# Attention layer and state-space scan on one core: maxima of four heads side by side, results taken a step later, and the causal convolution folded into the projection's weights

## The chip, the cores and the metric

The kernel runs on one core of a Trainium2 chip. The metric is the device time of one execution in microseconds (us); three executions of the kernel before gave 13804.61, 13823.3 and 13835.7 us, so the median is 13823.3 us. One more execution was taken with the hardware profiler; all rows shown here are from that one.

The engines are named as in the profile: PE is TensorE's matrix product and PEld its load of stationary weights, DVE is VectorE, ACT is ScalarE, POOL is GpSimd, and SP is SyncE, which issues the DMAs of this kernel. Each engine works through its own queue in order. PSUM, the memory into which products go, has eight banks of 128 partitions by 512 float32.

## The reference, cut to what matters

There are 16 samples of 256 channels by 32 x 32 positions (L = 1024), in float32. Each goes through two layers, each with a residual and a group norm before it.

```python
# layer 0: attention, 4 heads of 32
tok = gn(x) + pos_embedding
q, k, v = split(layernorm(tok) @ w_qkv)
attn = softmax(q k^T * 32**-0.5)              # 1024 x 1024 for each head
tok = (attn v) @ w_out + b_out + tok
tok = gelu(layernorm(tok) @ w_ff1 + b_ff1) @ w_ff2 + b_ff2 + tok
x = x + tok

# layer 1: a selective scan, 512 inner channels, 64 states
xp = gn(x) + rel_h + rel_w
ctx = sigmoid(conv3(xp, gate_w) + gate_b)     # dense convolution along positions
u, z = split(xp @ in_proj_w.T)
u = silu(causal_conv4(u, conv_w) + conv_b)    # each channel alone, 4 taps
dt, Bm, Cm = split(u @ x_proj_w.T)
delta = softplus(dt @ dt_proj_w.T + dt_proj_b)
h[t] = exp(delta[t] * A) * h[t-1] + delta[t] * u[t] * Bm[t]   # 512 x 64 states
y[t] = sum over states of h[t] * Cm[t]
x = x + ((y + u * D) * silu(z)) @ out_proj_w.T * ctx
```

## The kernel before, in words

**The scan sets the frame.** The 512 x 64 states of a sample are cut into 256 *units* (list `units`, L805). A unit is two scans of 128 partitions by 512 positions on VectorE (`scan`, L864). Each needs, ahead of it, a decay: a product on TensorE into a PSUM tile `a` (L851) and an exponential on ScalarE (L854), and an input: a DMA of `dub` (L832), 512 KB as it is repeated over partitions, and a product on POOL (L842). Loads are issued six units ahead, POOL's products four, decays two; `a` has four PSUM banks (pool `aps`), so the decays of a unit wait for the scans of two units earlier. Every eight units `outputs` sums over the states with 128 small products into `yb` (L901) and turns the result (L913).

**Preparation runs beside the scan.** While sample b is scanned, a chain of Python generators issues the work of other samples: `first_norm(b + 1)`, `gate_and_store(b - 1)`, `attention_layer(b + 1)` and `scan_inputs(b + 1)`, in this order. Each `yield w` ends a step of weight w. The loop over units (L946) adds a fixed share of the total weight for each unit and issues as many steps as are due. So a weight has no duration: it says how many units, and with them how much of the scan's work, are placed in each engine's queue before the next step's work. `add_manual_dep` at the end (L1001) keeps every engine's queue except SP's in this written order; SP's DMAs are ordered by the scheduler. The first sample is prepared alone, before the first scan (0 to 392 us); the last `gate_and_store` comes after the last scan.

**PSUM beside the scan.** `psum()` (L98) gives preparation the two banks of pool `mm`; pool `accp` has one bank (`av`), used by attention's sums. While the first sample is prepared alone, `psum()` takes turns through `mm` and `aps`.

**The parts that the change touches.**
- `group_norm` (L225) and `layer_norm` (L266): sums or means by products with `avg` on TensorE, then Ln and Exp on ScalarE, then a product on VectorE in a later step (L262, L301). Means of the two halves (L270) are used by VectorE (L277) one step later.
- `attention_layer` (L332): for each pair of heads, `query_key` (L363) projects q and k to rows 0-31 and 64-95 of `qa` and `ka`; 16 double steps compute scores `s_ps` (L408) of 128 queries by 512 keys for each head of the pair, and VectorE takes their maxima (L399) in the next step. The negated maxima are turned into rows by products with one column (`row_ps`, L420) and become row 32 of `qa`, against a row of ones in `ka`, so that the scores `st_ps` (L444) come with the maximum taken off. Then follow exponentials (L452) and the sums with the values (L432).
- `scan_inputs` (L537): z (L580), the tanh of silu and a product (L569) one step later; u (L601), copied to `up`, three taps on VectorE (L615; the fourth is the scale of a ScalarE copy, L607), a tanh and a product (L655); between them the dense gate (L630, L634); then x_proj (L667) and softplus with its split into bfloat16 pieces (L684 to L736).
- `gate_and_store` (L743): output projection `m_ps` (L789), finished by two VectorE operations (L776, L778) half a double step later.
- `spread_c` (L873): once for each half of a sample's positions, eight ScalarE copies (L880) into `cd`, which POOL sets to zero first (L876), once a sample.

## Time and profile before

| what | value |
|---|---|
| median of three executions | 13823.3 us |
| the profiled execution | 13784.86 us |
| its span, first to last instruction | 13782.7 us |
| mean granted TensorE clock | 0.732 |
| busy: DVE, PE, POOL, ACT | 88%, 81%, 76%, 59% |
| before the first scan | 392 us |
| scans of the first sample | 805 us |
| scans of samples 2 to 15 | about 847 us each |
| scans of the last sample, nothing prepared beside it | 677 us |
| one scan of 512 positions (L864) | 1201 to 1261 ns |
| one tap (L615), 192 in all | 1567 ns |
| one reduction of scores (L399), 1024 in all | 678 ns |
| DMA traffic | 2804 MB, 201 GB/s of HBM traffic over the span |

How to read the profile: a row of groups gives line, engine, operation, the tiles written and read, how often, busy time, mean duration, and the idle time of the engine just before with what ended it. A row of waits gives the instruction that waited, what it waited for, the total in us, how many times, the longest. A row of windows gives the length of a stretch and the busy time of each engine in it, then the share of TensorE's clock that was granted (1.00 is full speed), the share of the DMA engines in use, and GB/s. A float32 product stands in the profile as two records. The duration of a matmul is modelled at its end, and matmuls overlap, so TensorE's busy time says that it had work, not that it was at its peak.

### The profile page before, as it was taken

The page shows a single profiled execution, that of the slowest core. Times are in us where ns is not written, and L with a number is a line of the kernel's source. Part 1 is how long each engine was busy: PE and PEld are TensorE (multiplying, and loading weights), DVE is VectorE, ACT ScalarE, POOL GpSimd, SP SyncE. Part 2 cuts the span into 40 slices and gives each one's busy share as a digit, 9 for nine tenths or more (in the row PEclk, how much of TensorE's full clock was granted, in tenths as well). Part 3 has the DMA queues.
Part 4 walks back from the last instruction along what each step waited for, and adds up shares of the span by engine and source line. Part 5 has one row for each costly group of instructions (what it writes and reads, how often), then busy time and mean ns, then how long its engine had stood idle before and what let it go on. Part 6 is the DMA issues. An engine that isn't in the chain of part 4 may idle for free. (4 is left out here: it accounts for less than half of the span.)

```text
span 13782.7 us, 435036 instructions
## 1 busy us (share of the span) xinstructions
PE 11113.2 (81%) x185744; PEld 5728.7 (42%) x185744; DVE 12135.5 (88%) x11699; ACT 8088.7 (59%) x14245; POOL 10477.2 (76%) x8214
## 2 busy tenths in 40 slices
PE   7787878878787787978879788797887978878767
PEld 3344444444444444444444444444444444434434
DVE  3898898898898889888898888889888898888898
ACT  3666665656655565655656655566555655556644
POOL 0787777777787777777777787777777777777788
PEclk8686767867777686876767777677776776867767
DMA  1566566565665656556565565656656565565666
GB/s 55 196 207 230 187 214 208 201 222 196 211 207 199 218 201 223 194 199 218 197 231 186 197 226 191 232 185 202 219 191 230 187 214 205 194 228 187 209 219 223
DMA packets 964174, 2804.18 MB, mean 203 GB/s; under 512 B 138162, under 2 KB 285747, under 8 KB 962228
## 3 DMA queue, kind: packets, MB, share of 16 engines
q1 hardware_dynamic: 962228, 2776.34, 58.8%
q8 instruction: 1452, 23.79, 0.7%
q14 instruction: 494, 4.05, 0.1%
HBM read 2514.18 MB, written 261.62 MB: 201 GB/s over the span
## 5 line engine op out<-in xcount | busy, mean ns | idle before, releaser
L842 POOL TENSOR_TENSOR dub<-dub,bt 128x512 f32<-128x512 f32 x8192 | 10422.4, 1307 | 3254.5 <-DMA dub<-dus 2878.4
L854 ACT ACTIVATE a<-a,acol 128x512 f32<-128x512 f32 x8192 | 5064.9, 660 | 3728.2 <-PE a L851 3689.1
L864 DVE TENSOR_TENSOR_SCAN h<-a,last,dub 128x512 f32<-128x512 f32 x4096 | 4932.9, 1261 | 227.0 <-POOL dub L842 128.8
L864 DVE TENSOR_TENSOR_SCAN h<-a,dub 128x512 f32<-128x512 f32 x4096 | 4700.9, 1201 | 276.7 <-POOL dub L842 186.6
L851 PE MATMUL a<-pieces,pick 48*128 48x512 bf16 x8192 | 2914.9, 480 | 2103.1 <-DVE h L864 2037.8
L901 PEld LDWEIGHTS yb<-h,cd 128*32 128x32 f32 x131072 | 2677.2, 140 | 2166.2 <-issue 1847.3
L901 PE MATMUL yb<-h,cd 128*32 128x64 f32 x131072 | 3090.5, 265 | 160.9 <-DVE yb L891 115.9
L851 PEld LDWEIGHTS <-pick 48*128 48x128 bf16 x8192 | 498.0, 96 | 2507.4 <-issue 2293.2
L408 PE MATMUL s_ps<-ka,qa 32*128 32x512 f32 x2048 | 1115.7, 1009 | 23.2 <-DVE mx L399 15.2
L399 DVE TENSOR_REDUCE mx<-s_ps 128x1 f32<-128x512 f32 x1024 | 654.9, 678 | 279.0 <-PE s_ps L408 278.2
L913 PEld LDWEIGHTS yb<-turn,y 128*16 128x16 f32 x32768 | 418.9, 120 | 960.3 <-ACT y L909 484.6
L909 ACT COPY y<-yb 128x256 f32<-128x256 f32 x1024 | 383.4, 374 | 693.6 <-PE yb L901 688.3
L913 PE MATMUL yb<-turn,y 128*16 128x32 f32 x32768 | 555.2, 216 | 193.8 <-ACT y L909 173.0
L444 PE MATMUL st_ps<-qa,ka 33*128 33x512 f32 x2048 | 590.2, 613 | 25.9 <-ACT pt L452 25.5
L432 PE MATMUL av<-pt,vv 128*64 128x512 f32 x2048 | 572.7, 635 | 4.3 <-ACT sums L390 3.3
L452 ACT ACTIVATE pt<-st_ps 128x512 f32<-128x512 f32 x1024 | 558.9, 609 | 28.8 <-PE st_ps L444 28.4
L408 PEld LDWEIGHTS s_ps<-ka,qa 32*128 32x128 f32 x2048 | 345.4, 274 | 402.3 <-DVE mx L399 221.4
L630 PE MATMUL g_ps<-w,xp 128*128 128x256 f32 x1536 | 475.2, 468 | 0.0
L630 PEld LDWEIGHTS g_ps<-w,xp 128*128 128x128 f32 x1536 | 401.9, 329 | 137.6 <-issue 92.6
L789 PE MATMUL m_ps<-w,xs 128*128 128x256 f32 x1024 | 316.7, 459 | 10.9 <-DVE xs L764 10.9
L921 ACT COPY yo<-yb 128x256 f32<-128x256 f32 x512 | 193.1, 377 | 222.2 <-PE yb L913 219.7
L615 DVE SCALAR_TENSOR_TENSOR u<-up,cwh,u 128x1024 f32<-128x1024 f32 x192 | 300.9, 1567 | 23.8 <-ACT u L607 23.6
(135 smaller groups left out, 7593.8 us busy)
## 6 DMA issues: line engine op xcount, KB each, us to landing
dub<-dus SPq DMA_DIRECT2D x4096, 512.0 KB
dps<-pc SPq DMA_DIRECT2D x384, 128.0 KB
pieces<-dps SPq DMA_DIRECT2D x1024, 48.0 KB
xs<-in_x_dram SPq DMA_DIRECT2D x64, 512.0 KB
xs<-kept SPq DMA_DIRECT2D x64, 512.0 KB
zs<-z SPq DMA_DIRECT2D x64, 512.0 KB
ud<-u SPq DMA_DIRECT2D x64, 512.0 KB
dus<-du SPq DMA_DIRECT2D x64, 512.0 KB
```

What stands on the lines that cost most here:

```text
L399: nc.vector.tensor_reduce(mx[:, e, c, hf : hf + 1], s, AX.X, ALU.max)
L408: nc.tensor.matmul(s, qa[r, ts(c, P)], ka[r, hs(hf)], start=True, stop=True)
L432: nc.tensor.matmul(av[ts(e, 2 * DH)], vv[j // (NJ // 2)][:, j % (NJ // 2), 2 * pair + e, :], pts[e], start=(j == 0), stop=(j == NJ - 1),)
L444: nc.tensor.matmul(s, ka[r, ts(j, P)], qa[r, hs(hf)], start=True, stop=True)
L452: nc.scalar.activation(pt, s, AF.Exp)
L630: nc.tensor.matmul(ps[:, ts(q, C)], xp[k][:, ds(first + t, P, 4)], wg_s[:, k, t, :], start=(i == 0), stop=False,)
L842: nc.gpsimd.tensor_tensor(v, v, blocks[b, t]["bt"], ALU.mult)
L851: nc.tensor.matmul(a, w, pieces[r], start=True, stop=True)
L854: nc.scalar.activation(a, a, AF.Exp, scale=acol[:, at : at + 1])
L864: nc.vector.tensor_tensor_scan(now["h", q % 2][:, 2 * i + e, :], decays[n][e], loaded[n][:, e, :], first, ALU.mult, ALU.add,)
L901: nc.tensor.matmul(yb[ts(g, 32), ts(s, 64)], cd[:, at // 16, ts(c, 32)], hbuf[:, :, at : at + 4], start=(c == 0), stop=(c == 3),)
L913: nc.tensor.matmul(out4[32 * s : 32 * s + 16, half, e], y2[:, 64 * s + e : 64 * s + 64 : 4], turn[:, e], start=True, stop=True,)
```

## The change

1. *Maxima.* `query_key` is gone. q and k of all four heads are projected into `q4` and `k4`, head h in rows 32h to 32h + 31. Each of 32 steps issues four products, one for each head: 32 rows, 64 queries, 512 keys; two heads share a PSUM bank (partitions 0-63 and 64-127), and two banks hold the four. VectorE reduces the two banks in the next step, as before. The maxima are turned by one product, copied, and sent to `qa` by DMA. `qa` and `ka` of each pair are made from `q4` and `k4` by DMA (`spaced`), one to a step. The columns of w_qk are brought in an order that suits this (`bring_qk`). v's products come after the maxima instead of before.
2. *Results a step later.* A third bank (`accp`) joins `mm` through `psum3` for layer norm, z, u and m_ps; z's product, u's product and m_ps are finished one step later than before, and both halves' means are issued before VectorE uses the first. Weights of steps around exponentials are split and raised. `cd` is set to zero once, before everything, and its eight copies are spread over two units. In softplus the steps of the two halves are interleaved in another order.
3. *Convolution.* At the start POOL multiplies u's part of w_in by each of the four taps (halved, as before), and the products go to DRAM (`wcv`). u comes from eight products for each half, over four shifted views of the input, which is padded by three zeros; taps on VectorE and the copy `up` are gone. Each half is two steps of four products. The gate's products move from the convolution's steps to softplus's, in pieces of three.
4. *Room.* The weights' tile loses 1024 columns, and the pool `wide` has eleven buffers instead of ten. A_log is no longer kept.

```diff
-    wide = pool("wide", 10)
+    wide = pool("wide", 11)
...
+    three = cycle((mm, mm, accp))
+
+    def psum3(name):
+        src = next(three) if beside["scan"] else next(alone)
+        return src.tile([P, HL], F32, name=name, tag={mm: "mm", accp: "av"}.get(src, "a"))
...
+    cd = hst.tile([P, TB // 16, P], F32, name="cd", tag="cd")
+    nc.gpsimd.memset(cd, 0.0)
...
+    for d in range(ND):
...
+        t = work("wcs").rearrange("p (k t e) -> p k t e", k=KC, t=CONV)
+        for k in range(KC):
+            nc.gpsimd.tensor_tensor(
+                t[:, k], row[:, ts(d % 2, CONV * P)].rearrange("p (t e) -> p t e", t=CONV),
+                wu[:, k, ts(d, P)].unsqueeze(1).to_broadcast([P, CONV, P]), ALU.mult,
+            )
+        nc.sync.dma_start(wcv[ts(d, P), :], t.rearrange("p k t e -> p (k t e)"))
...
         nc.scalar.activation(v, v, AF.Exp, scale=-0.5)
-        yield 1.5
+        yield 1.2
+        yield 1
...
-        m = mean_of([t[:, hs(0)] for t in src], "ln_m")
-        yield 1
-        q0 = centre(0, m)
-        m = mean_of([t[:, hs(1)] for t in src], "ln_m")
+        m0 = mean_of([t[:, hs(0)] for t in src], "ln_m")
+        yield 0.7
+        m1 = mean_of([t[:, hs(1)] for t in src], "ln_m")
+        yield 0.7
+        q0 = centre(0, m0)
         yield 1.2
-        q1 = centre(1, m)
         vs = [mean_of(q0, "ln_v")]
+        q1 = centre(1, m1)
         yield 1.2
         vs.append(mean_of(q1, "ln_v"))
-        yield 1
+        yield 0.8
...
-        yield 2
+        yield 1.3
+        yield 1
...
+        def spaced(to, src, pair):
+            t = work("sp")
+            for e in range(2):
+                nc.sync.dma_start(t[ds(2 * DH * e, DH)], src[ts(2 * pair + e, DH)])
+            to.append(t)
...
+        for c in range(2 * NJ):
+            for hf in range(2):
+                maxima()
+                for g in range(2):
+                    waiting.append((psum("s_ps"), g, c, hf))
+                for h in range(HEADS):
+                    g, e = divmod(h, 2)
+                    r = ts(h, DH)
+                    nc.tensor.matmul(
+                        waiting[g][0][ts(e, 64)], q4[r, ts(c, 64)], k4[r, hs(hf)],
+                        start=True, stop=True,
+                    )
+                if to_space:
+                    to_space.pop(0)()
+                yield 1.1
...
+        ps = psum("neg_ps", HEADS * NJ)[:, :P]
+        nc.tensor.matmul(ps, neg, ident, start=True, stop=True)
+        yield 1.2
+        negt = small.tile([P, P], F32, name="negt", tag="negt")[: HEADS * NJ]
+        nc.scalar.copy(negt, ps)
+        for h in range(HEADS):
+            pair, e = divmod(h, 2)
+            o = 2 * DH * e + DH
+            nc.sync.dma_start(qas[pair][o : o + 1], negt[ts(pair, 2 * NJ), ts(e, 64)])
+        yield 0.7
...
         for d in range(ND):
             z = work("z")
             for hf in range(2):
-                finish_z()
-                ps = psum("z_ps")
+                finish_z(1)
+                ps = psum3("z_ps")
...
-            for k in range(KC):
+            w = wcs[d].rearrange("p (k t e) -> p k t e", k=KC, t=CONV)
+            ps = psum3("u_ps")
+            for i in range(KC * CONV):
+                k, t = divmod(i, CONV)
                 nc.tensor.matmul(
-                    ps, win_s[:, k, ts(d, P)], body[k][:, hs(hf)],
-                    start=(k == 0), stop=(k == KC - 1),
+                    ps, w[:, k, t], xp[k][:, ds(hf * HL + t, HL)],
+                    start=(i == 0), stop=(i == KC * CONV - 1),
                 )
...
+                if i == CONV - 1:
+                    yield 1.3
+            t = hwork("u_t")
+            nc.scalar.activation(t, ps, AF.Tanh, bias=cbh[:, d : d + 1])
+            nc.scalar.activation(ps, ps, AF.Identity, bias=cbh[:, d : d + 1])
+            ready.append((d, hf, t, ps))
-        def tap(d, t):
-            i = d * CONV + t
-            u = us[d]
-            nc.vector.scalar_tensor_tensor(
-                u, ups[d][:, t : t + L], cwh[:, i : i + 1], u, ALU.mult, ALU.add
-            )
...
-            items = [more(d, *items[0]), begin(d, 1)]
-            yield 1
+            items[0] = more(d, *items[0])
+            yield 0.8
+            items.append(begin(d, 1))
+            rest(*items[0])
+            yield 1.3
             items[1] = more(d, *items[1])
-            rest(*items[0])
-            yield 1.4
+            yield 0.8
             rest(*items[1])
...
+            gate(d // 2, d % 2, 0, 0)
             yield 1.4
...
-                ps = psum("m_ps")
+                ps = psum3("m_ps")
...
-                    if q == 0:
+                    if q == 1:
                         finish()
...
-        if (k, q, i) == (0, 0, 6):
-            spread_c(b, t)
+        if (k, q) == (0, 0) and i in (5, 6):
+            spread_c(b, t, ((0, 1), (2, 3))[i - 5])
```

## Prediction

> **What bounds the kernel now.** I read the busy shares first, then VectorE's waits from the first scan to the last (392 to 13737 us), then one sample cut into stages, then TensorE's clock in the stretch before the first scan, where one kind of work runs alone.
>
> ```profile
> PE 11113.2 (81%) x185744; PEld 5728.7 (42%) x185744; DVE 12135.5 (88%) x11699; ACT 8088.7 (59%) x14245; POOL 10477.2 (76%) x8214
> ```
>
> VectorE is busiest, but 12% of its time is idle. The fifteen samples that carry preparation beside their scan take about 847 us each (805 for the first); the last one, with almost none, took 677 (13060 to 13737). So preparation costs some 170 us a sample, and that is what the change touches. Who keeps VectorE waiting (name waited for: total us, times, longest):
>
> ```profile
> DVE h L864 <- POOL dub L842: 315.5, 287, 9.9
> DVE mx L399 <- PE s_ps L408: 209.5, 215, 2.6
> DVE h L864 <- issue: 177.9, 254, 2.6
> DVE z L569 <- ACT z_t L585: 107.6, 85, 2.7
> DVE gn L262 <- ACT gn_v_ps L259: 101.3, 15, 8.4
> DVE xn L301 <- ACT ln_v L296: 94.7, 30, 4.0
> DVE xn L277 <- PE ln_m L270: 76.6, 28, 4.7
> DVE d_ps L699 <- ACT d_ps L695: 75.4, 89, 1.7
> DVE m_ps L776 <- PE m_ps L789: 69.0, 56, 3.4
> ...
> DVE u L615 <- ACT u L607: 20.2, 15, 1.6
> ```
>
> Divided by 15, the waits of preparation (not L864) come to some 50 us a sample, of which the maxima's 14. Then the sample from 4572 to 5419 us by stages; columns: length, busy us of PE, PEld, DVE, ACT, POOL, granted clock, DMA share.
>
> ```profile
> 4597.00:4656.00 59.00, 32.84 (x672) 17.78 (x672) 50.05 (x44) 27.36 (x52) 48.56 (x35) 0.53 0.78 273
> ...
> 4738.00:4805.00 67.00, 63.91 (x739) 28.41 (x738) 56.43 (x66) 26.38 (x48) 41.80 (x34) 0.53 0.44 139
> ...
> 5181.00:5267.00 86.00, 75.46 (x1153) 48.25 (x1153) 79.35 (x64) 43.73 (x74) 66.48 (x48) 0.92 0.57 189
> 5267.00:5400.00 133.00, 96.55 (x1712) 46.63 (x1711) 124.22 (x128) 96.61 (x163) 91.69 (x75) 0.62 0.62 208
> ```
>
> The first row is the end of the group norm with the gate's first products: VectorE lacks 9 us. The second is a pair's maxima: TensorE is busy 63.9 of 67 at a clock of 0.53, so it bounds, not VectorE. The third is convolution, fourth softplus: VectorE bounds both (79 of 86, 124 of 133). Each part of the change must be priced against its own stage's bound.
>
> **Maxima of four heads side by side.** Counts: before, 32 steps a sample, each two 32-row products and two reductions; after, 32 steps, each four 32-row products of 64 columns and two reductions. Reductions (678 ns) stay 64. If the four products run together, TensorE streams as long per step as now. So all hangs on the clock. Three rows from the stretch where TensorE had nothing else:
>
> ```profile
> 80.00:95.00 15.00, 14.04 (x32) 5.08 (x28) 11.19 (x19) 0.00 (x0) 0.00 (x0) 0.50 0.00 0
> 95.00:99.00 4.00, 3.95 (x19) 2.39 (x20) 0.00 (x0) 0.92 (x2) 0.00 (x0) 0.50 0.00 0
> 99.00:100.00 1.00, 1.00 (x8) 0.64 (x6) 0.00 (x0) 0.23 (x1) 0.00 (x0) 0.63 0.00 0
> 100.00:101.00 1.00, 1.00 (x11) 0.62 (x9) 0.00 (x0) 0.57 (x1) 0.00 (x0) 1.00 0.00 0
> ```
>
> Up to 94 us only s_ps runs, two products on 64 of 128 rows: TensorE is 94% busy and stays at 0.50. From 95.05 to 100.91 only row_ps runs, 128 rows by one column: the clock goes to 1.00 within that stretch, before st_ps starts. The second pair repeats it (0.50 to 174, 0.79 over 174 to 176, row_ps from 170.0 to 176). The Trainium skill ("TensorE: Matmul & The Clock Gate", Part 1) says that the clock follows how busy TensorE was in windows of some 3.4 us. By that rule the maxima's 94% should have been at full clock, occupancy does not change, and the gain here is nothing. The row contradicts it: filled rows decide, filled columns hardly. The new quads fill all 128 rows, so I expect a clock near the 0.96 of the st_ps stretch (4805 to 4867).
>
> That the four really overlap no row shows: before has two row groups at once (a pair starts 7 ns apart), or column groups (yb), never both. The same page (Part 3) states rows and columns compose, 10.6 times for 16 tiles; I take "together". At full clock, 8 units then cost TensorE 8 quads x 1.1 us (half of the pair's 2.08 at half clock, rounded up) + 8.5 for the scan's own (4 x 1.10 yb, 2 x 0.47 turns, 8 x 0.39 decays) = 17.3 us; VectorE 16 scans at 2.33 a pair = 18.6, + 16 reductions x 0.6 = 28.2. VectorE becomes the bound: about 28.7 against 33.5 in the row above (67 for its 16 units) and 30 in the second pair's stretch (4891 to 4921). Over four such groups, and with 32 row_ps products shrunk to one, I take **-9.5 us** a sample; 0 if the clock stays, as far as -14 (all of the wait).
>
> The eight spreading DMAs (128 KB each), four 1-row ones and split w_qk fetches are about 1.3 MB beside some 175 MB a sample; SP issues each in about 0.4 us, already waiting for scans 6692 us. They are hidden as long as st_ps, behind whose wait decays would queue, starts two steps (about 6 us) after the negated maxima are sent: v_ps was moved between.
>
> **Convolution in u's weights.** VectorE loses 12 taps x 1.567 = 18.8 us a sample; the last products change from 4 x 1.48 to 8 x 0.69 (same). TensorE gets 64 products instead of 16. Eight u_ps records (four products; each product is two records) took 3.70 us at full clock (296.85), so 64 cost 59.2 us, 44.4 more. The 27.6 us of gate products (8 times 3.18 + 0.69 less overlap) leave this stage for softplus. The program's order puts 24 products into each 8 units: 22.2 + 8.5 = 30.7 us of TensorE, while VectorE needs 19.2 + 3 x 0.69 = 21.3. **The bound crosses to TensorE.** For the 24 units of the third stage row: 59.2 + 3 z steps x 1.98 + 3 x 8.5 = 90.6 against 86 now; the 8 units after them fall from 28 (5267 to 5295) to about 26, since x_ps (14) stays and gates leave. Sum **+2 us**: the 18.8 us saved do not show. From both sides: -8 (TensorE's pieces overlap, z waits counted below go too) to +12 (decays queue behind a 3.7 us piece and the scan waits). Fetching weights adds four 512 KB DMAs less a 512 KB half of w_in: four more of the size of dub's 256, prefetched a whole d (5.6 of weight, 5 units) ahead.
>
> In softplus 8 gates of 3.4 us at full clock, near 6 at half, lie over 40 units whose TensorE is 96.6 of 133 busy at 0.62. VectorE still bounds: 0, or +5 if decays queue.
>
> **Results taken a step later.** All step weights sum to about 276 after, 281 before, over 247 units: one weight is 0.9 unit, 2.9 us.
> - Group norm: the 6.45 us wait at 4606 is a chain: POOL's L876 memset 3.58, then eight L880 copies 2.45 on ScalarE, then exponentials, two table loads of 1.28. The memset is gone, copies are split over two units, and the step grows by 0.7 of weight (2 us). 6.75 a sample to 1.5, second norm 2.6 to 0.6: -7.2.
> - z: a third PSUM buffer and one more step (2.9) cover waits of at most 2.7: 7.2 to 1, of which 2 lie in the convolution groups counted above: -4.5.
> - Layer norm: means start earlier by 0.4 and 0.7, exponentials get 0.3 more: 5.1 to 2.1 and 6.3 to 4.5: -4.8.
> - m_ps: finished one step later: 4.6 to 0.6: -4.
> - d_ps: slack changes from 1.0 and 1.4 of weight to 0.8 and 0.8, with fewer ScalarE operations ahead: 0, between -4 and +4.
> Together **-20.5**; below by half if the delay is only passed to the scans' own waits (L864, 33 us a sample), which no edit addresses.
>
> **Outside the loop.** Before the first scan: SP now stores four weight tiles, each behind two POOL products of about 1.3 us and the taps' round trip, ahead of x's first fetch (14.3 us today): +20. Maxima alone: 54 us at half clock become VectorE-bound, 32 x 1.29 = 41: -13, row_ps -9. u_ps +44, gates moved into idle TensorE time -28. Sum +14. Last sample: -4.
>
> **Sum.** -9.5 + 2 - 20.5 = -28 a sample; 14 x -28, -24 for the first (no m_ps), -4, +14 = -406 us. The profiled execution took 13784.9 us (span 13782.7), so 13379, 2.95% less. The median shown is 13823.3, 0.28% above it; the same share gives **13,415**.
>
> **Rivals.** *More is gained* (0.20): preparation's waits go wholly and TensorE's groups overlap better, about -46 a sample: 13,150. For it: the waits are short and many. Against: the bound crosses in convolution. *The clock stays or waits pass on* (0.14): no -9.5, half of -20.5, softplus +2: -6 to -15 a sample, 13,600 to 13,740. For it: the page's rule, and 0.5 clock wherever little runs. *Slower* (0.10): quads that share a PSUM bank run one after another, so the clock stays and a step costs four passes, 3.8 us, in place of 2.08: 32 x 1.7 = +54 against -18.5 elsewhere, +36 a sample, about 14,350. It decides once a step costs 0.6 us more than now (18.5 / 32). Against it: yb's four column groups write one bank 7 ns apart.
>
> **Numbers.** Forecast 0.55, own range 13,270 to 13,560. For 8 in 10 I leave out the slower case and the outer part of "more": 13,150 to 13,660. A measurement of this kernel tells about 0.2%. Faster 0.87, same 0.03, slower 0.10.
>
> **What would show it.** Right: clock above 0.85 in the maxima's stretch with VectorE over 93% busy; u_ps stretches with TensorE over 93% and VectorE under 80%; no wait of gn for its exponent over 3 us; m_ps and z waits under 20 us in total. Wrong: s_ps records starting a pass apart rather than nanoseconds, the maxima still near 0.55, or L864's waits for dub or issue growing by what the others lost.

## The result and the profile after

The changed kernel takes 13,620.9 us (four executions, 13,611.9 to 13,629.1) against 13,815.9 us for the kernel before on the same chip (13,804.6 to 13,835.7): ratio 0.9857, 95% interval 0.984 to 0.9874. It is faster by 195 us, where 400 were forecast. The time lies above the forecast's own range (13,270 to 13,560) and inside the wide one (13,150 to 13,660). It also lies in the range of the rival "the clock stays or waits pass on" (13,600 to 13,740), although the clock did not stay. The profiled execution has a span of 13,613.7 us, 169 less than before.

First the busy times of the page, then the rows of its groups that the change touched (line, engine, operation, tiles, shapes, count; busy us, mean ns; idle time just before, and what ended it).

```profile
PE 11139.6 (82%) x188338; PEld 5586.7 (41%) x188338; DVE 11853.9 (87%) x11491; ACT 7820.4 (57%) x13878; POOL 10297.0 (76%) x8207
...
L932 DVE TENSOR_TENSOR_SCAN h<-a,last,dub 128x512 f32<-128x512 f32 x4096 | 4934.3, 1262 | 548.7 <-POOL dub L910 369.5
L932 DVE TENSOR_TENSOR_SCAN h<-a,dub 128x512 f32<-128x512 f32 x4096 | 4707.2, 1203 | 336.2 <-POOL dub L910 223.0
...
L675 PE MATMUL u_ps<-xp,xs 128*128 128x512 f32 x2048 | 976.3, 622 | 21.7 <-DMA xs<-wcv 21.6
L442 PE MATMUL s_ps<-k,q 32*64 32x512 f32 x4096 | 889.8, 728 | 51.8 <-DVE mx L423 49.9
L423 DVE TENSOR_REDUCE mx<-s_ps 128x1 f32<-128x512 f32 x1024 | 645.7, 675 | 22.1 <-PE s_ps L442 22.0
```

VectorE's work fell by 282 us (12,135.5 to 11,853.9), but the span fell by only 169: VectorE now stands idle 113 us longer. The scans (L932, formerly L864) show where: 885 us of idle time stand before them. In the kernel before it was 504 us:

```profile
L864 DVE TENSOR_TENSOR_SCAN h<-a,last,dub 128x512 f32<-128x512 f32 x4096 | 4932.9, 1261 | 227.0 <-POOL dub L842 128.8
L864 DVE TENSOR_TENSOR_SCAN h<-a,dub 128x512 f32<-128x512 f32 x4096 | 4700.9, 1201 | 276.7 <-POOL dub L842 186.6
```

The waits of VectorE between the first scan and the last, in the changed kernel:

```profile
DVE h L932 <- POOL dub L910: 592.5, 339, 6.4
DVE h L932 <- issue: 262.7, 300, 5.5
DVE d_ps L758 <- ACT d_ps L754: 202.1, 120, 5.7
DVE u L664 <- ACT u_ps L683: 117.0, 72, 2.0
DVE xs L828 <- DMA xs<-ud: 72.9, 16, 6.1
...
DVE m_ps L844 <- PE m_ps L857: 24.7, 14, 1.8
...
DVE z L636 <- ACT z_t L651: 16.2, 31, 1.7
...
DVE mx L423 <- PE s_ps L442: 12.3, 23, 1.5
...
DVE gn L301 <- ACT gn_v_ps L297: 3.5, 14, 0.3
```

Every wait that the change aimed at has shrunk: maxima 209.5 to 12.3 us, gn 101.3 to 3.5, z 107.6 to 16.2, m_ps 69.0 to 24.7 (the prediction named under 20 us for m_ps and z). Four others have grown: the scans' own from 493 to 855 us, d_ps from 75.4 to 202.1, u from 20.2 to 117.0, the load of ud from 33.3 to 72.9. Now one sample (4580 to 5412 us) in stages. These rows are the end of the group norm, the maxima, the middle of the convolution, and softplus:

```profile
4605.00:4632.00 27.00, 16.64 (x336) 8.94 (x336) 26.70 (x22) 13.59 (x24) 18.88 (x16) 0.56 0.59 198
...
4743.00:4852.00 109.00, 97.48 (x1605) 36.96 (x1607) 108.85 (x127) 46.58 (x86) 80.52 (x66) 0.89 0.54 181
...
5163.00:5226.00 63.00, 62.33 (x777) 29.12 (x776) 43.14 (x40) 29.01 (x52) 39.30 (x32) 1.00 0.56 181
...
5255.00:5370.00 115.00, 88.18 (x1448) 52.16 (x1447) 102.33 (x107) 85.40 (x143) 79.08 (x64) 0.76 0.62 205
```

In the maxima the clock is 0.89 and VectorE is busy 108.85 of 109 us: the bound crossed from TensorE to VectorE, as forecast. In the convolution it crossed the other way: TensorE 62.33 of 63 us, VectorE 43.14. Averaged over samples 3 to 15, each sample's 256 units cut by unit number into the same stages:

| stage, us a sample | before | after | change | forecast |
|---|---|---|---|---|
| group norm, results stored (units 0 to 47) | 167.0 | 159.7 | -7.3 | -11.2 |
| maxima and attention (48 to 135) | 270.9 | 257.7 | -13.2 | -9.5 |
| layer norms, feed forward, z (136 to 175) | 144.0 | 134.0 | -10.0 | -9.3 |
| convolution (176 to 207) | 114.0 | 123.0 | +9.0 | +2 |
| softplus (208 to 239) | 110.4 | 115.7 | +5.3 | 0 |
| rest | 41.6 | 41.4 | -0.2 | 0 |
| sum | 847.9 | 831.5 | -16.4 | -28 |

The 11.6 us missing stand in convolution and softplus (12.3 together); the other stages give 30.5 where 30.0 were forecast. The cut is by unit number, and the steps do not stand at quite the same units in both kernels: beside the scan of one sample, u's products lie in units 179 to 194 before and 182 to 200 after. So a few microseconds can stand in a neighbouring stage. The first scan comes at 422.9 us (392.7 before: +30, forecast +14), and the first sample's scans take 821 us (805: +16, forecast -24).

### The profile page after: what moved, and what is told of

It is laid out like the page before. It is cut to its first block, busy times and chain, and to the rows that moved or that the text cites. A ratio compares the mean times of both kernels' runs of the same rounds, so it can differ in the third digit from the quotient of the medians.

```text
span 13613.7 us, 440125 instructions
## 1 busy us (share of the span) xinstructions
PE 11139.6 (82%) x188338; PEld 5586.7 (41%) x188338; DVE 11853.9 (87%) x11491; ACT 7820.4 (57%) x13878; POOL 10297.0 (76%) x8207
## 5 line engine op out<-in xcount | busy, mean ns | idle before, releaser
L910 POOL TENSOR_TENSOR dub<-dub,bt 128x512 f32<-128x512 f32 x8192 | 10283.0, 1288 | 3243.4 <-DMA dub<-dus 2846.8
L932 DVE TENSOR_TENSOR_SCAN h<-a,last,dub 128x512 f32<-128x512 f32 x4096 | 4934.3, 1262 | 548.7 <-POOL dub L910 369.5
L932 DVE TENSOR_TENSOR_SCAN h<-a,dub 128x512 f32<-128x512 f32 x4096 | 4707.2, 1203 | 336.2 <-POOL dub L910 223.0
L919 PE MATMUL a<-pieces,pick 48*128 48x512 bf16 x8192 | 2728.5, 452 | 1915.9 <-DVE h L932 1886.8
L966 PEld LDWEIGHTS yb<-h,cd 128*32 128x32 f32 x131072 | 2495.5, 132 | 1834.3 <-issue 1676.3
L966 PE MATMUL yb<-h,cd 128*32 128x64 f32 x131072 | 2889.6, 254 | 71.3 <-issue 67.2
L675 PE MATMUL u_ps<-xp,xs 128*128 128x512 f32 x2048 | 976.3, 622 | 21.7 <-DMA xs<-wcv 21.6
L442 PE MATMUL s_ps<-k,q 32*64 32x512 f32 x4096 | 889.8, 728 | 51.8 <-DVE mx L423 49.9
L510 PE MATMUL st_ps<-sp 33*128 33x512 f32 x2048 | 614.7, 634 | 15.1 <-DMA sp<-negt 7.3
L675 PEld LDWEIGHTS u_ps<-xp,xs 128*128 128x128 f32 x2048 | 380.8, 195 | 490.9 <-issue 447.4
L696 PE MATMUL g_ps<-w,xp 128*128 128x256 f32 x1536 | 558.9, 513 | 9.6 <-ACT g L704 9.6
L442 PEld LDWEIGHTS s_ps<-k,q 32*64 32x64 f32 x4096 | 201.9, 147 | 552.2 <-DVE mx L423 513.3
```

The lines of the kernel that those rows point to most:

```text
L442: nc.tensor.matmul(waiting[g][0][ts(e, 64)], q4[r, ts(c, 64)], k4[r, hs(hf)], start=True, stop=True,)
L510: nc.tensor.matmul(s, ka[r, ts(j, P)], qa[r, hs(hf)], start=True, stop=True)
L675: nc.tensor.matmul(ps, w[:, k, t], xp[k][:, ds(hf * HL + t, HL)], start=(i == 0), stop=(i == KC * CONV - 1),)
L696: nc.tensor.matmul(ps[:, ts(q, C)], xp[k][:, ds(first + t, P, 4)], wg_s[:, k, t, :], start=(k == 0 and t == 0), stop=False,)
L910: nc.gpsimd.tensor_tensor(v, v, blocks[b, t]["bt"], ALU.mult)
L919: nc.tensor.matmul(a, w, pieces[r], start=True, stop=True)
```

## The experiments

**Theory.** The clock in the maxima follows filled rows; the missing gain was lost in softplus's new order and in the convolution's and gates' work on TensorE. **Rivals.** The delays only move the waits on to the scans; or the fetch of the folded weights, not TensorE's work, fills the convolution; or it is only the places of steps against units that shifted. Ratios are against the kernel before, on the same chip.

### The clock: rows filled with zeros

```diff
+                nc.sync.dma_start(ka[2 * DH * e + DH : 2 * DH * (e + 1)], ones)
+                nc.sync.dma_start(qa[2 * DH * e + DH : 2 * DH * (e + 1)], zeros)
...
-                        r = ds(2 * DH * e, DH)
+                        r = ds(2 * DH * e, 2 * DH)
```

The kernel before, with rows 32 to 63 of each head's half of q zero (those of k zero but for one row of ones), so that its scores contract over 64 rows. Work, order and results stay; the two products of a pair now fill 128 rows with half of them nothing.

> The kernel before, with one thing changed: rows 32 to 63 of each head's half of qa and ka hold zeros (ones in row 32 of ka) while the maxima are taken, and the scores' products contract over 64 rows instead of 32. Same number of products, same columns, same result; four row groups are filled instead of two. Theory 'rows decide the clock': granted clock in the maxima's stretches rises from about 0.55 to over 0.8, VectorE's wait for s_ps falls from 14 us a sample to under 3, time falls by 8 to 12 us a sample, 120 to 190 us in all: 13,630 to 13,700. Rival 'occupancy decides the clock' (or zeros do not count as work): clock there stays at 0.55 and the time within 0.2% of before, 13,790 to 13,840.

Measured: 13,652.6 us, 0.9882 (0.9861 to 0.9902). The two stretches of a sample's maxima, by windows:

```profile
4694.00:4753.00 59.00, 51.92 (x739) 23.42 (x738) 55.40 (x64) 25.53 (x47) 41.28 (x34) 0.81 0.47 166
4815.00:4867.00 52.00, 46.31 (x735) 20.35 (x732) 48.83 (x54) 30.09 (x55) 42.37 (x36) 0.90 0.58 208
```

The first pair's 16 units took 67 us at a clock of 0.53 before, and 59 at 0.81 here. The stage of maxima and attention falls from 270.9 to 261.0 us a sample, and no other stage moves by over 0.7. Rows of zeros alone save 158 us: what counts for the clock here is that rows are filled.

### Each part alone

The kernel before with the maxima of four heads (and A_log no longer kept, which makes the room); with the results taken a step later, softplus's new order included; with the convolution in u's weights and the gates in softplus. No arithmetic is left out.

> The kernel before with the maxima of four heads side by side alone (first part of the change, and A_log's columns loaded apart to make room). Theory 'each part acts on its own stage': the stretch of maxima and attention loses 13 us a sample as in the changed kernel, 15 x 13 = 195 us less, 13,620 +- 40. Rival 'the gain is the removed row_ps and copies, not the clock': then zero_rows is near 13,815 while this one still gains 150 or more. Rival 'the eight spreading DMAs hold up the loads': a wait of POOL for dub grows by over 5 us a sample in this stretch and the gain is under 100 us.

> The kernel before with the results taken a step later alone: third PSUM bank for layer norm, z and m_ps, later steps, cd zeroed once and spread over two units, softplus in the new order; maxima and convolution as before. Forecast of record for this part: -20.5 us a sample. From the trace of the changed kernel I now expect about -17 in group norm, layer norm, z and m_ps, less some 3 to 8 given back in softplus by the new order: -9 to -14 a sample, 13,605 to 13,680. Rival 'softplus loses only because gates moved there': no loss in softplus here, d_ps waits stay at 5 us a sample, and the time is 13,560 to 13,600.

> The kernel before with the convolution in u's weights alone (eight products for each half, u finished a step later over three banks, gates moved into softplus's steps); maxima, norms, z, m_ps, cd and softplus's order as before. Theory 'the bound crosses to TensorE and the steps are too small': 10 us a sample more in the convolution's groups and 0 to 5 more in softplus, plus about 35 us before the first scan: 13,815 + 190 +- 90, so 13,910 to 14,090, slower than before. Rival 'convolution gains about what its taps cost, and something else in the change loses': 13,560 to 13,700.

Measured: maxima 13,554.5 us, 0.9818 (0.9796 to 0.9839); later results 13,706.8, 0.9927 (0.9906 to 0.9948); convolution 13,970.5, 1.0118 (1.0096 to 1.014), its first scan at 453 us. The three changes of time, -256, -104 and +160, add to -200, close to the -195 of the whole. That is luck, as the next runs show: maxima and later results together save not 360 us but 105. Of the 256, the 158 of the zero rows are the clock; the other 98 come with the rest of that part (row_ps gone, steps at other units) and were not taken apart. Only 11.1 of its 15.1 us a sample lie in its own stage, 3.9 in the convolution's units. The convolution alone loses, by 7 us in its own units (121.0 against 114.0) and 6.6 in softplus (117.0 against 110.4); and later results, new order included, give a third of the 307 us (15 x 20.5) forecast.

### Softplus's order

```diff
-            items[0] = more(d, *items[0])
-            yield 0.8
-            items.append(begin(d, 1))
-            rest(*items[0])
-            yield 1.3
-            items[1] = more(d, *items[1])
-            yield 0.8
+            items = [more(d, *items[0]), begin(d, 1)]
+            yield 1
+            items[1] = more(d, *items[1])
+            rest(*items[0])
+            yield 1.4
             rest(*items[1])
```

First the changed kernel without its convolution part, then the same with softplus's old order, then the whole changed kernel with the old order.

> The changed kernel with its third part undone: taps on VectorE, whole gates between them, w_in whole, ten wide buffers; maxima and later results stay. If the parts act on their own stages, it gains what the two alone gained (256 + 104 us): 13,455, between 13,410 and 13,500, and so is faster than the changed kernel by 165. Rival 'the parts need each other' (the convolution makes room in VectorE that the later steps use): no faster than the changed kernel, 13,600 or more.

> As no_conv, and softplus's steps in the order of before. In late_only the wait of d_ps for ScalarE was 9.6 us a sample against 5.0 before. Theory 'the new order gives d_ps too little slack': 4 to 5 us a sample less than no_conv, 60 to 75 us. Rival 'the wait only stands for time that passes elsewhere': within 20 us of no_conv.

> The changed kernel with softplus's steps in the order of before; gates stay in softplus. In the changed kernel d_ps waits 13.4 us a sample, in conv_only (old order, gates) 12.5, in late_only (new order, no gates) 9.6, before 5.0. Theory 'the gates on TensorE and ScalarE cause most of it': 1 us a sample, 0 to 30 us less than the changed kernel. Rival 'the order causes it': 70 us or more less.

Measured: 13,708.3 us, 0.9914 (0.9891 to 0.9938); 13,536.5, 0.9795 (0.9779 to 0.9811); 13,507.8, 0.9779 (0.976 to 0.9799). The first was expected at 13,410 to 13,500: the parts do not simply add. The old order gains 172 us without the convolution and 113 with it, where 60 to 75 and nothing to 30 were expected. With it, the whole change takes 13,507.8 us, inside the forecast's own range. Maxima and later results without the convolution save 276 us, and the convolution on top no longer costs anything (29 us less, within the two intervals). But the maxima alone saved 256: on top of them, later results bring 20 us, which is within the intervals too (0.9818 and 0.9795). But the new order also weighs 2.9 in place of 2.4, which moves every other step against the units. Two runs separate order and place: the new order with weights 0.6, 1.2 and 0.6, and the old with 1.2 and 1.7.

> The changed kernel with softplus's new order kept, but its three steps weigh 0.6, 1.2 and 0.6 of weight, together the 2.4 of the old order instead of 2.9. So every step of the sample stands at the same unit as in the run with the old order (13,508 us), and only the order inside softplus differs from it. If the order itself costs the time (half an item's exponential is not done when VectorE comes for it): shorter slack makes it worse, 13,620 to 13,720 us, with the d_ps wait above 14 us a sample. If the longer total, which moves all other steps against the units, cost the 113 us: about 13,510 us.

> The changed kernel with softplus's old order, its two steps weighing 1.2 and 1.7 of weight, together the 2.9 of the new order. Every other step stands where it does in the changed kernel. If the order itself costs the time: 13,480 to 13,520 us, and the d_ps wait falls below 12 us a sample through the longer slack. If the place of the other steps against the units does: about 13,620 us.

| us | weight 2.4 | weight 2.9 |
|---|---|---|
| old order | 13,507.8 | 13,564.1 |
| new order | 13,655.2 | 13,620.9 (the change) |

The order costs 147 us at one weight and 57 at the other; the weight moves the time by 56 up or 34 down. With weight 2.4 every other step stands at the same unit in both kernels, and softplus's units take 125.6 us against 116.8 while no other stage of the table differs by over 0.8. VectorE's waits show it, first with the old order, then with the new:

```profile
DVE d_ps L758 <- ACT d_ps L754: 176.8, 75, 7.3
```

```profile
DVE d_ps L758 <- ACT d_ps L754: 328.1, 120, 7.3
```

The new order makes VectorE come at 120 places instead of 75 before ScalarE has finished the half's Relu (L754): 151 us more waiting, about the 147 us of time. At weight 2.9 the change waits 202.1 us there, and the old order 80.4 us, at 62 places. That is 122 us more waiting for the new order, of which 57 arrive in the time. In the change itself the greater weight hid part of the wait (softplus 115.7) and gave it away elsewhere: convolution +3.9 us, layer norms and z +3.4, against the run with weight 2.4.

### Weights of the convolution's steps doubled

```diff
                 if i == CONV - 1:
-                    yield 1.3
+                    yield 2.6
...
                 finish_u(1)
-                yield 1.5
+                yield 3.0
```

> The changed kernel with the weights of the convolution's steps doubled (2.6 and 3.0 in place of 1.3 and 1.5), nothing else: the same products beside some 37 units of scan instead of 20. Theory 'in its 20 units TensorE is the bound (59 us of products + 1.06 a unit) while VectorE idles 8 us in each 8 units': each of the 17 units that move in costs TensorE 1.1 us here and frees about 2.4 us of VectorE elsewhere, so up to 20 us a sample less, 150 to 300 us in all: 13,320 to 13,470. Rival 'the stage is slow because pieces of 3.7 us delay decays and inputs, whatever the share': no gain, within 60 us of 13,620, or slower as other stages get less cover.

Measured: 13,777.7 us, 0.9968 (0.9953 to 0.9982), 157 us slower than the change, as the rival had it, and not faster by 150 to 300. The convolution's products now lie over about twice the units, its old 32 units take 97.0 us instead of 123.0, but everything else is denser: attention (units 80 to 135) takes 167.0 us (148.1 in the change), the group norm's stage 166.9 (159.7). So room made for the convolution was taken from the other stages. Whether any stretch could take TensorE's 44 us more for nothing is not shown by this.

### Results a step later, without the order

The kernel before with the later results and softplus's old order; then the same with the sum of the first norm and the position embedding made by POOL.

```diff
-            nc.vector.tensor_tensor(tok[k], tok[k], gn[k], ALU.add)
+            nc.gpsimd.tensor_tensor(tok[k], tok[k], gn[k], ALU.add)
```

> The kernel before with the results taken a step later, but with softplus's old order. The prediction's -20.5 us a sample without the order would be 13,812 - 15 x 20.5 = about 13,505 us. If the order costs here what it did in the kernel without the convolution (172 us): 13,707 - 172 = 13,535. If the delays only pass the waits on to the scans' own waits: above 13,640, and the scans' waits for POOL and issue rise by over 10 us a sample.

> The kernel before with the results a step later and softplus's old order (13,653 us), with one edit: the two sums of norm and embedding of each sample are made by POOL instead of VectorE. If these sums waited inside their own time for POOL's products: VectorE loses 2 x 4.26 us a sample, 13,653 - 15 x 8.5 = about 13,525 us, less if dub comes later by POOL's 2 x 2.5 us. If not: between 13,620 (their plain 2 x 1.2) and 13,690 us (POOL's delay of dub).

Measured: 13,653.0 us, 0.988 (0.9866 to 0.9895), and 13,572.6, 0.9828 (0.9808 to 0.9849). In the first, the waits named in the prediction fell by 320 us (z, gn, xp, both of xn, m_ps), 21.3 a sample where 20.5 was forecast. The time fell by 154. Part of the rest is in a row that shows no idle time; VectorE's groups in that run:

```profile
L343 DVE TENSOR_TENSOR xs<-xs,gn 128x1024 f32<-128x1024 f32 x30 | 127.8, 4259 | 0.0
```

In the kernel before:

```profile
L328 DVE TENSOR_TENSOR xs<-xs,gn 128x1024 f32<-128x1024 f32 x30 | 38.3, 1277 | 0.0
```

It reads two tiles of SBUF, and it now falls where POOL multiplies without a pause. Moved to POOL:

```profile
L343 POOL TENSOR_TENSOR xs<-xs,gn 128x1024 f32<-128x1024 f32 x32 | 75.7, 2367 | 30.1 <-DVE gn L275 30.1
```

Units 8 to 15 of a sample fell from 29.9 to 20.7 us, 9.2 where 8.5 was expected; but units 16 to 23 rose from 30.7 to 35.5, and no other 8 units changed by over 0.7. There the next operation of VectorE waits for loads; first with the sum on POOL, then in the run before it:

```profile
DVE xs L776 <- DMA xs<-ud: 73.3, 26, 9.2
...
DVE xs L776 <- DMA dub<-dus: 49.6, 6, 8.6
```

```profile
DVE xs L776 <- DMA xs<-ud: 39.8, 26, 3.5
...
DVE xs L776 <- DMA dub<-dus: 15.4, 5, 3.4
```

So half of the 9.2 us was handed to the next thing that is late. With the sum out of the way, the version is 238 us below the kernel before, 15.9 a sample; up to 2.6 of that is the two sums themselves, which VectorE no longer makes.

### The first sample

```diff
+    x0 = [work("xs") for _ in range(KC)]
+    for k in range(KC):
+        nc.sync.dma_start(x0[k], x[0][ts(k, P), :])
     wcv = dram1.tile([ND * P, KC * CONV * P], F32, name="wcv", tag="wcv")
```

> The changed kernel with softplus's old order (13,508 us), and the first sample's two fetches issued before the weights are multiplied by the taps. If the queue of SP is what makes the first sample late: x is fetched before 16 us, first scan about 20 us earlier (400 us), 13,488 us. If the stretch at half clock in its attention is the larger part: first scan 410 to 420 us and no change that can be told from 13,508.

Measured, on top of softplus's old order: 13,481.2 us, 0.9769 (0.9749 to 0.9788), against 0.9779 for the order alone; the first scan at 407.1 us in place of 419.8. The difference in time is within the two intervals; the trace shows 12.7 of the 20 us. It also gives a measure of chance: after the first sample nothing differs between these two kernels but the moment at which it starts, and yet the samples' mean is 822.8 us here and 826.2 there. Stage sums of one run can be compared to about 3 us, unless, as with the two orders, all other stages agree.

### The fetch of the weights, and the gates

```diff
             z = work("z")
+            if d == ND - 1:
+                fetch(wcs, wcv, 0)
...
-        fetch(wcs, wcv, 0)
         finish_z()
```

```diff
                 nc.scalar.activation(s, s, AF.Ln)
+            gate(d // 2, d % 2, 0, 0)
             yield 1.7
...
             if d + 1 < ND:
                 items = [begin(d + 1, 0)]
-            gate(d // 2, d % 2, 1, 1)
             yield 1.4
```

The first moves the first fetch ahead by two steps of z: in the changed kernel, and on top of the old order and the early input. The second shifts all four pieces of the gate one step earlier; then both together; then both with the norm's sum on POOL.

> The changed kernel with one edit: the first fetch of folded weights is issued two steps of z earlier (2 of weight, some 6 us). If the late fetch, with the clock and the loads of dub behind it, is what fills the convolution's waits: no wait of u_ps for its weights, VectorE's waits in the four convolution groups fall from 37 to about 27 us a sample, 13,621 - 15 x 8 = about 13,500 us. If those groups are bound by TensorE's work alone, as the forecast had it: no change, 13,590 to 13,640.

> The same edit of the fetch in the version with softplus's old order and the first sample's input fetched early (13,481 us). Late fetch as the cause: 8 to 10 us a sample, 13,330 to 13,370 us. TensorE's work alone: 13,460 to 13,500.

> The version with softplus's old order and the early input (13,481 us), each of the four pieces of the gate's products issued one step earlier, so that none stands in the step that begins the next d's softplus, between its products and their exponentials. If the gates delay those exponentials: the d_ps wait falls from 12 to below 7 us a sample, 13,390 to 13,420 us. If the d_ps wait has another cause: 13,460 to 13,500, the wait stays at 10 to 13.

> Both edits. If both causes hold and stand in different stages, their gains add: about 13,270 us. If the stages behind only pass them on to the scans' own waits: no more than the better of the two alone.

> The same edit in the version with softplus's old order, early input, early weights and shifted gates (13,428 us). If VectorE waited for POOL there: 2 x 1.2 us and the 5 us above it, 13,428 - 15 x 7.5 = about 13,315 us. If not: 13,390 to 13,460.

| kernel | us | ratio (95%) | softplus's units | convolution's units |
|---|---|---|---|---|
| the change, fetch early | 13,599.6 | 0.9863 (0.9846 to 0.988) | 117.0 | 120.5 |
| old order, early input (from above) | 13,481.2 | 0.9769 (0.9749 to 0.9788) | 115.5 | 119.3 |
| the same, fetch early | 13,431.5 | 0.9741 (0.9725 to 0.9758) | 117.2 | 114.1 |
| the same, gates shifted | 13,499.4 | 0.9792 (0.9778 to 0.9807) | 111.3 | 119.9 |
| both | 13,427.7 | 0.9741 (0.9726 to 0.9755) | 111.4 | 114.5 |
| both, sum on POOL | 13,410.3 | 0.9707 (0.9691 to 0.9724) | 111.0 | 114.7 |

The fetch was late: with the old order, TensorE waits for it once a sample, as its row of waits says.

```profile
PE u_ps L675 <- DMA xs<-wcv: 37.2, 15, 3.1
```

With the fetch early this wait is gone and the convolution's units shorten by 5.2 us in one version, by 2.5 in the changed kernel; there the total did not change (0.9857 to 0.9863), in the other it fell from 0.9769 to 0.9741, with intervals that overlap. In that one the convolution's units take as long as before the change (114.1 and 114.0): the fetch and what it delayed were all of their loss, and TensorE's work is why the 18.8 us of taps saved do not show as a gain. In the changed kernel 6.5 of the 9.0 us stay; 3.9 of the 9.0 are absent when softplus's weight is 2.4 instead of 2.9, in either order (119.1 and 119.4), so they are the places of the steps. The gates were in the way: shifted, the d_ps wait falls from 162.4 to 73.7 us, and softplus by 4.2 us. The total did not follow. As much, 4.3 us, came back in units 8 to 15, in the sum of the first norm and the position embedding. VectorE, then POOL, in that run in time (start, duration, engine, instruction):

```profile
5392.81 2.33 DVE L937 TENSOR_TENSOR_SCAN h<-a,dub 128x512 f32<-128x512 f32 x2
5395.06 6.99 DVE L376 TENSOR_TENSOR xs<-xs,gn 128x1024 f32<-128x1024 f32 x1
...
5404.22 1.19 DVE L376 TENSOR_TENSOR xs<-xs,gn 128x1024 f32<-128x1024 f32 x1
```

```profile
5389.88 11.08 POOL L915 TENSOR_TENSOR dub<-dub,bt 128x512 f32<-128x512 f32 x9
5406.98 2.49 POOL L915 TENSOR_TENSOR dub<-dub,bt 128x512 f32<-128x512 f32 x2 [6.01 <-DMA dub<-dus]
```

The first of the two sums is recorded with 6.99 us and ends 1.1 us after POOL's last product without a gap does (5400.97); the second, while POOL waits for a load, takes 1.19. With that sum on POOL the ratio falls by 0.0034 (0.9741 to 0.9707). In microseconds the run stands in the band for "not" of its expectation; but it ran on a chip whose kernel before took 13,810.6 us, and its forerunner on one with 13,781.5. By ratio the gain is about 47 us, less than half of the 113 expected. The stage says why: units 8 to 15 fell from 28.6 to 20.7 us, 7.9 where 7.5 was expected, and units 16 to 23 rose from 33.3 to 37.9, where the load of ud is late (138.4 us in all, 91.6 without the edit). This is the fastest version found, 2.9% below the kernel before.

## Why the prediction was right or wrong

- **Maxima, -9.5: right in mechanism, a little small.** The stage moved by -13.2 a sample, the part alone by 256 us. Clock 0.89, VectorE busy 99.9%, the wait 12.3 us: each as named. The rule weighed there, that the clock follows TensorE's busyness, would have given nothing; the zero rows decide against it in this case, since they change no busyness, only the rows, and save 158 us. That the four products run together was taken from two rows that each showed half of it, and held: all quads keep TensorE busy for 889.8 us, the pairs for 1115.7, or 966.5 with rows of zeros. How the 98 us beyond the clock's 158 come about was not tested.
- **Convolution, +2: the bound crossed as forecast, the fetch was put at nothing.** It took +9. The groups of 8 units full of products were put at 30.7 us of TensorE each; they take 30.9 and 31.4 (TensorE busy for 30.5 and 31.1), and 30.7 where z ends (27.4). The misses are the fourth group, put at 26 because the gates leave it, which takes 30.0, and "prefetched a whole d ahead", which is true of three fetches; the first came one step ahead, and that wait and what it delayed stand for 2.5 us in the change and 5.2 with the old order. The steps' new places, with the greater weight in softplus, stand for 3.9.
- **Gates in softplus, "0, or +5 if decays queue": the upper end was right, the queue another.** With the convolution, softplus's units grew by 6.6 us and 8.2 (alone, and on top of the rest with the old order). The exponentials of softplus queue behind the gates' products; shifted, 4.2 of it goes.
- **d_ps, "0, between -4 and +4": the step that failed most.** Softplus's edit, order and weights, costs 113 us: with the old ones the change takes 13,507.8 us, in the forecast's range. The order costs 57 to 147 us in all, 8.8 us a sample in softplus where all else stands at the same places. The working had the slack right (1.0 and 1.4 of weight before, 0.8 and 0.8 after) and priced its loss at nothing, counting on fewer ScalarE operations ahead; the waits of d_ps in the kernel before, 89 of at most 1.7 us, were a sign that there was no slack to give. In the change the step's greater weight hid a part of it in softplus and moved it into other stages.
- **Results a step later, -20.5: the waits went as forecast (21.3), their sum did not reach the end.** About 10 a sample arrived alone, 15.9 once the norm's sum was moved to POOL, and next to nothing clear of noise on top of the maxima (20 us in all). The prediction had this as a fear ("if the delay is only passed to the scans' own waits") and put it in a rival; it was passed instead to a sum that shares something with POOL, and to the loads of ud. In the table, group norm and m_ps gave 7.3 of 11.2, layer norms and z 10.0 of 9.3.
- **L864's waits growing was named as a sign of being wrong, and they grew by 362 us,** most of it in the convolution's 32 units (6.8 to 27.9 us a sample). There TensorE sets the pace (62.33 of 63 us), so VectorE's free time shows as waits of the scans.
- **Outside the loop, +14: it was +30.** SP's queue delayed x by 21.6 us (14.3 to 35.95), as forecast (+20). The rest is attention at half clock, shown below: from the first score to the last product with the values it takes 139.3 us (87.6 to 226.9) where it took 144.3 before (67.0 to 211.3), 5 us less and not 22. The first sample's scans were put at -24 and took +16, so that the first sample, with what stands ahead of it, is 56 us of the 206 missing: the convolution alone makes them 29 us longer than before. Why it costs more there than in a later sample was not tested.

With order, fetch and gates undone ("both"), a sample takes 820.4 us, where the forecast's -28 would have made it 819.9. That this agrees to half a microsecond is chance, given the 3 us above. That the order cost time is shown in the time; the shares of fetch and gates are shown in their stages only.

## What to carry to other kernels

Price a re-ordering of dependent steps by the slack of each pair of producer and consumer: where the profile of before already shows many short waits on that pair, a little slack taken away can be paid in full (151 us of waiting cost 147 us in one pair of runs, 122 cost 57 in the other). Do not add what parts save alone: here two parts saved 256 and 104 us alone, and 105 together. When a wait is taken away, look at what VectorE does next and which engine or load it shares: a gain is real only if that is early too. When work is moved to an engine that is half free on average, price it in the stage where it lands, with the first fetch of its operands.

## What the runs showed of the hardware

**The clock can stay at half for one run of work and be full for the same run.** While the first sample is prepared alone, the same products of attention run at either clock. Two products of st_ps (four records) and two of av, after the same pause of 1.65 us: first the kernel before, then the one with later results.

```profile
122.56 1.13 PE L444 MATMUL st_ps<-qa,ka 33*128 33x512 f32 x4
123.62 1.08 PE L432 MATMUL av<-pt,vv 128*64 128x512 f32 x4
```

```profile
122.11 1.82 PE L459 MATMUL st_ps<-qa,ka 33*128 33x512 f32 x4
123.86 1.98 PE L447 MATMUL av<-pt,vv 128*64 128x512 f32 x4
```

The sequence of instructions is the same; the second stands 0.45 us earlier in the execution. It stays slow for some 25 us (120 to 145), of which TensorE is busy 23.9. In the changed kernel this happens twice, by windows:

```profile
145.00:150.00 5.00, 5.00 (x20) 1.13 (x16) 0.00 (x0) 2.17 (x4) 0.00 (x0) 1.00 0.00 0
...
154.00:176.00 22.00, 22.00 (x48) 4.50 (x44) 0.00 (x0) 6.19 (x12) 0.00 (x0) 0.52 0.00 0
...
202.00:226.00 24.00, 24.00 (x52) 5.29 (x52) 0.00 (x0) 6.80 (x13) 0.00 (x0) 0.51 0.00 1
```

TensorE is busy for all of 154 to 176 us and the clock is 0.52; in 145 to 150 the same mix runs at 1.00. These 46 us at half clock cost some 23 us of the first sample. In these stretches, products of 33 rows alternating with products of 128 hold a full clock and do not win back one that is lost. Why the same pause loses it in one execution and not in the other was not found.

**VectorE waits inside its own time for POOL.** A sum of two SBUF tiles took 1.19 us while POOL stood still, and up to 6.99 us (9.2 in the run of later results with the old order) while POOL multiplied without a gap. The Trainium skill ("SBUF — State Buffer", section "SBUF: two separate sides") describes one pair of ports that POOL, or VectorE where it reads two tiles of SBUF, holds for a whole instruction while the other one is blocked. In the changed kernel this would fit 11 of the 15 first sums: they took 1.6 to 2.4 us, about one product of POOL (1.3 us) and the sum itself. The other four took 5.5 to 5.7 us and ended some 1.1 us after the last of several products without a gap. So VectorE is let in between two products of POOL at some times and at others only when POOL pauses; what decides it was not found. No wait row shows this: it appears as a longer mean of the instruction.
